# A graph layer on one core: message remainders moved to TensorE, wider comparisons on VectorE, and other edits to a planned schedule

## The chip, the cores and the metric

The kernel runs on one core of a Trainium2 chip. The metric is the time on the device in microseconds (us), the median of several runs. Besides, one execution was recorded by the hardware profiler; the profile's line numbers are those of the kernel's file.

## The reference, cut to what matters

There are 6250 nodes with 128 values each and 100000 edges, sorted by destination. Each edge takes its source's row, multiplies it by one of two weight matrices, according to its type, and adds a bias. The messages are summed by destination, the node's own row times a third matrix is added, and the sum goes through relu, a residual and a layer norm.

```python
Xs = X[src]
m_data = Xs @ W_data.T + b_data
m_ctrl = Xs @ W_control.T + b_control
msg = jnp.where((edge_types == 0)[:, None], m_data, m_ctrl)
agg = jax.ops.segment_sum(msg, dst, num_segments=X.shape[0])
out = agg + (X @ W_self.T + b_self)
x = _layernorm(x + relu(out))
```

## The kernel before, in words

**Blocks.** The nodes are cut into 49 blocks of 128. Sources fall into NT = 98 buckets: 49 blocks for each of the two edge types. A bucket of one destination block has R = 32 slots for its edges; edges beyond that are *spilled* and treated apart.

**First stage: the messages of all nodes.** The messages of every node under both matrices are computed once (`multiply`, L441 the bias, L444 the products), and kept in SBUF as `m3`, in three bf16 parts whose sum has the precision of float32. `split_x` cuts x into three such parts (L420 to L427), so a product takes nine matmuls of 256 columns for a block. The result y stands in PSUM, two blocks to a tile, and is cut into parts by `split_a` to `split_d`: ScalarE copies the first part (L456), VectorE subtracts it from y (L463), ScalarE copies the second (L469), GpSimd or VectorE subtracts again (L474). The table of messages and x's parts are also stored in HBM (`table`, `x3_t`).

**Second stage: where each edge goes.** Blocks are handled in ten groups (four blocks, then five each). For a group, `edge_fields` loads windows of 2304 edges, 18 per partition. For each of the 18 columns k, `bucket_hots` compares the edges' buckets with a count (L544, the tile hot_st); TensorE multiplies that by a triangular matrix (`tri`) into the accumulator `acc`; VectorE takes a maximum over the buckets, which is the edge's rank in its bucket (L561, `slot`); and TensorE adds the rest of the column (`rest`), so that the next column's ranks go on from there. So column k + 1 follows column k through TensorE, VectorE and TensorE. Every three columns (KC = 3), `fill_a` compares the ranks with the 32 slots and multiplies by the source's and destination's place (L574 to L582), and `fill_b` adds these up in PSUM (L600). `fill_c` then copies the filled slots (L613, L615), stores them in HBM (`packed`, L618), turns the destination places (L628, L633), and finds the spilled edges: L640 to L674 pick up to two for each block and partition, L657 and L659 number them, L679 to L699 write a list of up to 32 of them and their one-hot `hot_s`, and L701 fetches their messages from the table. L708 to L718 note whether a bucket or list ran over; then a second, general path follows that the given inputs don't take.

**Third stage: the sums.** For each block, `spread` broadcasts its slots from HBM over all partitions (rows, L733, four buffers), `select` turns them into a one-hot (L740), and `to_hots` makes one for the destinations, five sets at a time (DC = 5, L752, hot_d). Twenty-five times per block, four buckets at a time, `gather` fetches messages by matmul (L768, 128 columns by 384 in four side by side), ScalarE copies them out of PSUM (L777), and `add_up` sums them into the block's accumulator `agg` (L216). The last set has two buckets only, so 64 rows. `own_of` adds the node's own term, one set more the spilled edges. The accumulator has one PSUM buffer: the next block's sums start when `finish_parts` has reduced it (L139). `normalise` scales a group at its end, and stores it.

**The order of the work.** The kernel writes each engine's queue by hand, through a planner (`Order`): every piece of work is a `step` with an assumed cost for each engine that can do it, the steps it needs, and a due time from `due`. The planner takes, among the steps that can start about first, the one due earliest, and emits it. So assumed costs and due times decide the fixed order in which each engine gets its instructions; on the chip every engine goes through its own in that order. BUILT and BLOCK set the due times. `close_build` frees the first stage's SBUF and PSUM, after which the tiles of the third stage are allocated there, the rows among them: their load needs the step `built`.

Of the kernel before, what the change touches and what calls it, by code (L numbers as in the profile page):

```python
# [9 lines left out]
F32 = mybir.dt.float32  # L10
# [9 lines left out]
P = 128  # L20
D = 128
# [18 lines left out]
NC = 4 * NS  # L40
PARTS = (4, 8, 8, 8, 8, 8, 5)
KC = 3
DC = 5
# [54 lines left out]
def kernel(  # L98
# [38 lines left out]
    def finish_parts(h, agg, xs, work):  # L137
        whole = work.tile([P, D], F32, name="whole")
        nc.vector.tensor_reduce(whole, agg.rearrange("p (i c) -> p c i", i=3), axis=AX.X, op=ALU.add)  # L139
        finish(h, whole, xs)  # L140
# [51 lines left out]
    with ExitStack() as main:  # L192
        sums_over_windows(main, tc, x, xt, edges, w, bias, table, x3_t, packed, total,
                          finish_parts, load_rows, norm)
# [6 lines left out]
def sums_over_windows(ctx, tc, x, xt, edges, w, bias, table, x3_t, packed, total,  # L201
                      finish_parts, load_rows, norm):
# [3 lines left out]
    work = ctx.enter_context(tc.tile_pool(name="work", bufs=2))  # L206
    ps_a = ctx.enter_context(tc.tile_pool(name="ps_a", bufs=1, space=PSUM))
# [13 lines left out]
    w_sb = const.tile([D, D3], F32, name="w_sb")  # L221
    A.dma_start(w_sb, w)
    b3 = const.tile([3, D3], F32, name="b3")
    A.dma_start(b3, bias.to_broadcast([3, D3]))
# [22 lines left out]
    V.tensor_scalar_add(slot_f, iota_f[:, :R], 256.0)  # L247
# [19 lines left out]
    early = ctx.enter_context(ExitStack())  # L267
    build = early.enter_context(tc.tile_pool(name="build", bufs=2))
    ps_y = early.enter_context(tc.tile_pool(name="ps_y", bufs=YB, space=PSUM))
# [6 lines left out]


    tri = const.tile([P, P], BF16, name="tri")
    rest = const.tile([P, P], BF16, name="rest")
    tri_f = work.tile([P, P], F32, name="tri_f", bufs=1)  # L280
    V.tensor_scalar(tri_f, iota_f[:, :P], pid, None, op0=ALU.is_gt)
    V.scalar_tensor_tensor(tri_f, ident, 256.0, tri_f, op0=ALU.mult, op1=ALU.add)
    V.tensor_copy(tri, tri_f)
    V.tensor_scalar(rest, tri_f, -1.0, 1.0, op0=ALU.mult, op1=ALU.add)
    ident_b = const.tile([P, P], BF16, name="ident_b")
    V.tensor_copy(ident_b, ident)

    slot_values = []
    for i in range(2):
        vs = const.tile([P, (Q + 1) // 2, NC], BF16, name=f"vs{i}")  # L290
        V.memset(vs, 0.0)
        slot_values.append(vs)
    fifth = const.tile([P, 2, Q], F32, name="fifth")
    for i in range(2):
        V.tensor_scalar_add(fifth[:, i, :], iota_f[:, :Q], 1.0)
# [9 lines left out]
    left = work.tile([D, D3], F32, name="left", bufs=1)  # L305
    three_parts([w3[:, i, :] for i in range(3)], w_sb, left)
    parts = work.tile([3, 3, D3], BF16, name="parts", bufs=1)
    three_parts([parts[:, i, :] for i in range(3)], b3, left[:3])


    spill_tiles = []
    for i in range(2):
        hot = const.tile([P, Q * P], BF16, name=f"hot_s{i}")
        V.memset(hot, 0.0)
        V.memset(hot[R : R + 1, :], 1.0)
        msg = const.tile([P, D3], BF16, name=f"msg_s{i}")
        V.memset(msg, 0.0)
        V.tensor_copy(msg[R : R + 1, :].rearrange("p (i c) -> p i c", i=3), parts[0:1, :, 2 * D :])
        spill_tiles.append((hot, msg))
    bias3 = const.tile([3, D3], BF16, name="bias3")  # L320
    V.tensor_scalar_mul(left[:3], parts[:, 0, :], ident[:3, 0:1])
    for i in (1, 2):
        V.scalar_tensor_tensor(left[:3], parts[:, i, :], ident[:3, i : i + 1], left[:3],
                               op0=ALU.mult, op1=ALU.add)
    V.tensor_copy(bias3, left[:3])
    order.free["V"] = 7.0

    first = const.tile([1, NB], I32, name="first")
    counts = const.tile([P, NPG], F32, name="counts")
    win = const.tile([P, NB, KT, 3], I32, name="win")  # L330
# [3 lines left out]
    def starts():  # L334
        yield step("counted", {"V": 1.8}, lag=0.3)
        dst_f = build.tile([NB, ER], F32, name="dst_f", bufs=1)
        V.tensor_copy(dst_f, er[:, :, 1])
        less = build.tile([NB, ER], F32, name="less", bufs=1)
        in_row = work.tile([NB, 1], F32, name="in_row")
        V.tensor_scalar(less, dst_f, bound_p, None, op0=ALU.is_lt, op1=ALU.add, accum_out=in_row)  # L340
# [7 lines left out]
        for b in range(NB):  # L348
            grp = [g for g in range(NPG) if STARTS[g] <= b][-1]
            yield step(("win", b), {"S": 0.84}, "first", *([("fields", grp - 2)] if grp > 1 else []),  # L350
                       lag=2.0)
            at = nc.values_load(
# [4 lines left out]
                win[:, b, :, :], edges[ds(at, WIN), :].rearrange("(p k) c -> p k c", p=P)  # L357
# [3 lines left out]
    x3s, xts, ys, lefts = {}, {}, {}, {}  # L361
# [6 lines left out]
    BLOCK = 13  # L368
    AHEAD = 12.0

    def due(kind, *i):
# [10 lines left out]
        if kind in ("y", "yh", "yr", "ym", "yl"):  # L382
            return LEAD + each * i[0] + ("y", "yh", "yr", "ym", "yl").index(kind)
        if kind in ("table", "x3_t"):
            return LEAD + each * (at_part[i[0]] + PARTS[i[0]]) + 6
        if kind in ("win", "xs", "agg", "o", "sum"):
# [4 lines left out]
            return begun + (BLOCK + 1 if kind == "sum" else 0.3 * BLOCK)  # L391
        if kind in ("rows", "sel", "d", "g", "e", "s"):
            of = {"rows": 1, "sel": 1, "d": 5}.get(kind, NS)
# [3 lines left out]
        end = BUILT + BLOCK * STARTS[i[0]] - AHEAD  # L397
        begun = end - BLOCK * n
        if kind == "fields":
            return begun - 8  # L400
        if kind in ("hot", "tri", "rank", "rest"):
            return begun + BLOCK * n * i[1] / KT + {"hot": -4, "tri": 0, "rank": 0.5, "rest": 1}[kind]
# [577 lines left out]
```

## Time and profile before

| | |
|---|---|
| time, median of 3 runs | 758.0 us (757.65 to 758.0) |
| span of the profiled execution | 755.7 us |
| TensorE matmuls busy | 694.5 us, 92% |
| TensorE weight loads busy | 553.7 us, 73% |
| VectorE busy | 645.1 us, 85% |
| ScalarE busy | 563.0 us, 74% |
| GpSimd busy | 58.5 us, 8% |
| first / last gather (L768) | 116.5 us / about 743 us |
| DMA | 73.09 MB, a mean of 97 GB/s |

PE is TensorE's matmuls and PEld its weight loads, DVE VectorE, ACT ScalarE, POOL GpSimd, SP the engine that issues most DMAs. A line of a group gives its source line, engine, operation, what it writes from what, the shape and count, then busy time and mean ns of one, and the idle time of the engine just before it with what ended that idle time. "issue" stands for a wait that the profile doesn't explain. Matmuls overlap in pipeline and in the four column strips of the array, so a busy TensorE isn't one at its peak; what tells more is the time from one set's start to the next one's.

### The profile page before, as it was taken

Reading aid. Unit: us, or ns where it says so; the run is one execution under the profiler, and the core shown is the slowest. Engines: PE = TensorE matmul, PEld = TensorE weight load, DVE = VectorE, ACT = ScalarE, POOL = GpSimd, SP = SyncE. Lnnn points to the kernel's source line nnn. Section 1 sums busy time; section 2 is a strip of 40 time slices with the busy share of each in tenths; the row PEclk is TensorE's granted clock in tenths of the full one; section 3 lists DMA queues with packets and bytes.
Section 4 is the critical chain, followed back from the end, with each engine's and each line's share of the span. In section 5 each row is a group of like instructions: output and inputs, shape, how many; then the busy total and the mean of one; then the engine's idle time right before and its main releaser. Section 6 shows DMA issues by size and latency. Waiting matters only on the chain.

```text
span 755.7 us, 34248 instructions
## 1 busy us (share of the span) xinstructions
PE 694.5 (92%) x14578; PEld 553.7 (73%) x14578; DVE 645.1 (85%) x1683; ACT 563.0 (74%) x1379; POOL 58.5 (8%) x48
## 2 busy tenths in 40 slices
PE   0989948999999999999999999999999999999993
PEld 0556636787887888788688778868878887888772
DVE  8798878999999989999999999899989999968531
ACT  1545425788888888778887878878787887789994
POOL 2454420000000000000000000000000000000000
PEclk9999977999999999999999999999999999999997
DMA  5456564024105213410521431052042014105200
GB/s 206 126 175 189 173 199 153 19 82 140 59 21 188 77 23 104 157 27 16 185 77 29 157 102 24 23 195 63 18 183 82 12 53 168 65 12 189 71 4 22
DMA packets 57572, 73.09 MB, mean 97 GB/s; under 512 B 12294, under 2 KB 50195, under 8 KB 57363
## 3 DMA queue, kind: packets, MB, share of 16 engines
q1 hardware_dynamic: 55806, 66.70, 27.2%
q10 hardware_dynamic: 1158, 3.41, 1.3%
q8 instruction: 116, 1.90, 1.0%
q0 software_dynamic: 448, 0.72, 0.3%
q14 instruction: 44, 0.36, 0.2%
HBM read 52.85 MB, written 17.96 MB: 94 GB/s over the span
## 4 chain that ended last, share of the span: by engine, by line
PE 66%; DVE 28%; DMA 2%; issue 2%; ACT 1%; POOL 0%; ACTq 0%; DVEq 0%
PE agg L216 24%; PE g_ps L768 20%; PE acc L216 9%; PE small L600 6%; PE y L444 6%; DVE slot L561 4%; DVE hot_d L752 4%; DVE hot_st L544 2%; DVE two L582 2%; DVE whole L139 2%; DMA rows<-packed 1%; DVE hr L577 1%; DVE rows L740 1%; PE y L441 1%; DVE st L149 1%
## 5 line engine op out<-in xcount | busy, mean ns | idle before, releaser
L777 ACT CAST gs<-g_ps 128x384 bf16<-128x384 f32 x1225 | 493.8, 500 | 114.2 <-PE g_ps L768 79.5
L768 PE MATMUL g_ps<-m,rows 128*32 128x384 bf16 x4802 | 412.1, 331 | 5.9 <-DVE rows L740 5.9
L216 PE MATMUL agg<-gs,hot_d 128*32 128x384 bf16 (+1 forms) x4900 | 412.7, 331 | 1.8 <-ACT gs L777 1.6
L768 PEld LDWEIGHTS <-rows 128*32 128x32 bf16 x4802 | 241.3, 136 | 41.8 <-issue 15.3
L216 PEld LDWEIGHTS <-hot_d 128*32 128x32 bf16 (+1 forms) x4900 | 225.8, 115 | 37.9 <-issue 21.0
L752 DVE TENSOR_TENSOR hot_d<-count,to 128x640 bf16<-128x640 bf16 x245 | 133.0, 553 | 13.6 <-PE agg L216 10.9
L561 DVE TENSOR_REDUCE slot<-acc 128x5 f32<-128x490 f32 (+1 forms) x180 | 116.8, 649 | 17.3 <-PE acc L216 11.4
L544 DVE TENSOR_TENSOR hot_st<-count,st_b 128x640 bf16<-128x640 bf16 (+1 forms) x180 | 100.0, 573 | 0.5 <-PE small L600 0.5
L216 PE MATMUL acc<-hot_st,rest 128*32 128x490 bf16 (+1 forms) x720 | 82.6, 375 | 12.2 <-DVE slot L561 10.8
L216 PE MATMUL acc<-hot_st,tri 128*32 128x490 bf16 (+1 forms) x720 | 89.8, 371 | 2.7 <-DVE full L708 2.7
L600 PE MATMUL small<-hot_st,two 128*32 128x100 bf16 x1764 | 76.1, 294 | 3.4 <-DVE two L582 2.6
L600 PEld LDWEIGHTS <-two 128*32 128x32 bf16 x1764 | 62.9, 119 | 10.6 <-DVE two L582 9.2
L444 PE MATMUL y<-w,x 128*128 128x256 bf16 x441 | 59.7, 282 | 0.4 <-POOL x L427 0.4
L139 DVE TENSOR_REDUCE whole<-agg 128x128 f32<-128x384 f32 x49 | 27.2, 555 | 38.3 <-PE agg L216 29.7
L701 POOL DMA_INDIRECT msg_s<-table,row_i x10 | 13.3, 1330 | 573.9 <-PE g_ps L768 507.8
L216 PEld LDWEIGHTS <-rest 128*32 128x32 bf16 x720 | 32.8, 97 | 28.3 <-issue 25.4
L740 DVE TENSOR_SCALAR rows<-rows,pid 128x3136 bf16<-128x3136 bf16 x49 | 50.4, 1028 | 0.2
L444 PEld LDWEIGHTS <-x 128*128 128x128 bf16 x441 | 39.9, 100 | 12.2 <-POOL x L427 0.9
L216 PE MATMUL agg<-w,x_p 128*32 128x384 bf16 x588 | 37.2, 326 | 0.0
L469 ACT CAST m<-yr 128x512 bf16<-128x512 f32 (+1 forms) x25 | 15.2, 609 | 26.9 <-DVE yr L463 26.7
L216 PEld LDWEIGHTS <-tri 128*32 128x32 bf16 x720 | 30.3, 97 | 6.0 <-issue 4.0
L582 DVE TENSOR_TENSOR two<-hr,lo 128x480 bf16<-128x480 bf16 (+1 forms) x60 | 29.0, 484 | 2.1
(140 smaller groups left out, 462.0 us busy)
## 6 DMA issues: line engine op xcount, KB each, us to landing
rows<-packed SPq DMA_DIRECT2D x49, 784.0 KB, 6.7
table<-m SPq DMA_DIRECT2D x10, 768.0 KB, 7.1
x_p<-x_t SPq DMA_DIRECT2D x49, 96.0 KB, 2.3
x_t<-x SPq DMA_DIRECT2D x5, 768.0 KB, 4.6
xs_p<-in_x SPq DMA_DIRECT2D x49, 64.0 KB, 2.1
xt<-in_xt ACTq DMA_DIRECT2D x5, 512.0 KB, 5.9
out<-h_p SPq DMA_DIRECT2D x8, 320.0 KB, 2.5
win<-in_edges SPq DMA_DIRECT2D x49, 27.0 KB, 2.1
```

What stands on the lines that cost most here:

```text
L139: nc.vector.tensor_reduce(whole, agg.rearrange("p (i c) -> p c i", i=3), axis=AX.X, op=ALU.add)
L216: T.matmul(out[c : c + 32], lhsT[:, c : c + 32], rhs, **flags)
L444: T.matmul(y[:, j, :], x3s[g][:, b + j - at_part[g], i, :], w3[:, k, : 2 * D], start=False, stop=i == k == 2)
L469: A.copy(parts_of(b, n)[1], lefts[b])
L544: V.tensor_tensor(hot, counted[n], fields[grp][2][:, k, None, :].to_broadcast([P, P, n]), op=ALU.is_equal)
L561: V.tensor_reduce(slots[grp][:, k, :], by_q, axis=AX.X, op=ALU.max)
L582: V.tensor_tensor(two[:, :, i], hr, f[:, ks, None, :].to_broadcast(wide), op=ALU.mult)
L600: T.matmul(vt[c0 : c0 + R, q // 2, :], two[:, k - c * KC, i, :, q], hot[:, :, q], start=k == 0 and q < 2, stop=k == KT - 1, skip_group_che ...
L740: V.tensor_scalar(rows[b], rows[b], pid1, None, op0=ALU.is_equal)
L752: V.tensor_tensor(hot, counted[DC], places[grp][:, q, None, c * DC : c * DC + DC].to_broadcast([P, P, DC]), op=ALU.is_equal)
L768: T.matmul(g_ps[t * R : (t + 1) * R, :D3], rows[b][:, :, 4 * g + t], m3[:, 4 * g + t, :], start=True, stop=True)
L777: (A.copy if e == "A" else V.tensor_copy)(gs[:n], g_tiles.pop((b, g))[:n, :D3])
```

## The change

The edits, in the order of the program:

- **Constants and bias.** The bias row is cut into three parts on one partition and spread to a tile of 128 rows, so that its matmul has 128 rows like the others (before: three). The constants are made in a planned step (`constants`) behind the first x remainder. `win` gets two buffers in place of one tile for all blocks; w and other early tiles lie in the pool that is freed.
- **Remainders on TensorE.** `take` and `leave` replace `split_a` to `split_d`: after each part is copied by ScalarE straight from PSUM, TensorE subtracts it there by a matmul with minus the identity. VectorE and GpSimd have no part in it any more. x's third part is always VectorE's.
- **Wide comparisons.** hot_st is made for six columns at once (KC = 6) and for the 98 buckets alone, hot_d for 13 or 12 sets at once (DC = 13), with one count of 13.
- **bf16 ranks.** Ranks count from SLOT = 128 in place of 256, so that they and the slots are exact in bf16, and `at` falls away. The last column's `rest` isn't computed.
- **Spilled edges by the eight largest.** One comparison and one instruction for the eight largest codes of a partition replace the reductions for two per block; eight flags for up to ten; the reduction of `acc` falls away.
- **The last gather of a block** repeats a bucket to fill four, so all sets have 128 rows.
- **The sums' PSUM freed early.** `finish_parts` is cut into `whole` (the reduction out of PSUM) and `sum`; the plan lets the next accumulator start after `whole`.
- **Rows in their own pool**, so their load doesn't need `built`.
- Planned costs and due times are changed throughout (BLOCK 13.5 for 13, group 0 is due 12 us earlier).

The core of the diff:

```diff
-KC = 3
-DC = 5
+RB = 4
+M = 8
+SLOT = 128.0
+KC = 6
+DC = 13
...
+    row_pool = ctx.enter_context(tc.tile_pool(name="row_pool", bufs=RB))
...
-            free = [("yr", two_blocks[i - YB][1])] if i >= YB else []
-            yield step(("y", b), {"T": 1.2 * n}, ("x3", g), *free)
+            free = [("yl", two_blocks[i - YB][1])] if i >= YB else ["biased"]
+            yield step(("y", b), {"T": 1.08 * n}, ("x3", g), *free)
...
-                T.matmul(y[:, j, :], ones_b[:3, :], bias3[:, : 2 * D], start=True, stop=False)
+                T.matmul(y[:, j, :], ones_b, bias3, start=False, stop=True, skip_group_check=True)
...
+    def take(i, kind, after):
         for g, b, n in two_blocks:
+            yield step((kind, b), {"A": 0.16 + 0.21 * n}, (after, b))
+            A.copy(part_of(b, n, i), ys[b][:, :n, :].rearrange("p b (t c) -> p t b c", t=2))
+
+    def leave(i, kind, after):
         for g, b, n in two_blocks:
+            yield step((kind, b), {"T": 0.11 * n}, (after, b))
+            for j in range(n):
+                T.matmul(ys[b][:, j, :].rearrange("p (t c) -> p t c", t=2), minus,
+                         m3v[:, :, b + j, i * D : (i + 1) * D], start=False, stop=True,
+                         skip_group_check=True)
...
-            V.tensor_tensor(hot, counted[n],
-                            fields[grp][2][:, k, None, :].to_broadcast([P, P, n]), op=ALU.is_equal)
+            V.tensor_tensor(hot, counted[n][:, None, 1 : NT + 1, :].to_broadcast([P, KC, NT, n]),
+                            fields[grp][2][:, c * KC : c * KC + KC, None, :].to_broadcast([P, KC, NT, n]),
+                            op=ALU.is_equal)
...
+                if k == KT - 1:
+                    break
                 yield step(("rest", grp, k), {"T": 0.21}, ("rank", grp, k))
...
-                at = work.tile([P, KC, Q], BF16, name="at")[:, :, :n]
-                V.tensor_scalar_add(at, slots[grp][:, ks, :], -256.0)
...
+                V.tensor_tensor(hr, slot_b[n][:, None, :, :].to_broadcast(wide),
+                                slots[grp][:, ks, None, :].to_broadcast(wide), op=ALU.is_equal)
...
+            V.scalar_tensor_tensor(over.rearrange("p (k q) -> p k q", q=n), slot, SLOT + R, code,
+                                   op0=ALU.is_ge, op1=ALU.mult)
+            last = work.tile([P, M], F32, name="last", bufs=1)
+            V.max(last, over)
...
-            V.tensor_reduce(full, accs.pop(grp)[:, : n * NT], axis=AX.X, op=ALU.max)
...
-            yield step(("rows", b), {"S": 0.1}, ("packed", grp), "built", *free, lag=4.0)
-            rows[b] = late.tile([P, R, NT], BF16, name="rows", bufs=RB)
+            yield step(("rows", b), {"S": 0.1}, ("packed", grp), *free, lag=4.0)
+            rows[b] = row_pool.tile([P, R, NT], BF16, name="rows")
...
+            hot = late.tile([P, P * DC], BF16, name="hot_d", bufs=DB)[:, : P * n]
+            d_hots[b, c] = hot = hot.rearrange("p (s g) -> p s g", g=n)
+            V.tensor_tensor(hot, counted[DC][:, :, :n],
+                            places[grp][:, q, None, c * DC : c * DC + n].to_broadcast([P, P, n]),
                             op=ALU.is_equal)
...
-            for t in range(n // R):
-                T.matmul(g_ps[t * R : (t + 1) * R, :D3], rows[b][:, :, 4 * g + t],
-                         m3[:, 4 * g + t, :], start=True, stop=True)
+            for t in range(4):
+                s = min(4 * g + t, NT - 1)
+                T.matmul(g_ps[t * R : (t + 1) * R, :D3], rows[b][:, :, s], m3[:, s, :],
+                         start=True, stop=True)
...
-            yield step(("agg", b), {"S": 0.0}, *([("sum", blocks[i - 1])] if i else []))
+            yield step(("agg", b), {"S": 0.0}, *([("whole", blocks[i - 1])] if i else []))
```

## The prediction

> **What bounds the kernel now.** First the busy tenths over the span (page, part 2), one digit per fortieth:
>
> ```profile
> PE   0989948999999999999999999999999999999993
> ...
> DVE  8798878999999989999999999899989999968531
> ACT  1545425788888888778887878878787887789994
> POOL 2454420000000000000000000000000000000000
> PEclk9999977999999999999999999999999999999997
> ```
>
> TensorE is nearly always busy, but VectorE is too (645.1 of 755.7 us). TensorE has one hole, its sixth slice (94 to 113 us); at the end VectorE is free and ScalarE full. The view by windows of 20 us (TensorE, weight loads, VectorE, ScalarE, GpSimd, clock, DMA) gives the hole and a steady stretch:
>
> ```profile
> 100.00:120.00 20.00, 7.63 (x123) 4.31 (x124) 17.93 (x54) 4.06 (x10) 2.97 (x3) 0.62 0.82 268
> ...
> 280.00:300.00 20.00, 20.00 (x501) 17.87 (x494) 18.26 (x57) 17.56 (x46) 0.00 (x0) 1.00 0.21 62
> ```
>
> Three engines are close together, so I asked what TensorE waits for (waits view: who for whom, us in total, times, longest):
>
> ```profile
> PEld L216 <- issue: 59.0, 182, 2.7
> ...
> PEld L441 <- issue: 11.2, 49, 0.4
> ...
> PE acc L216 <- DVE slot L561: 10.8, 21, 2.0
> ...
> PE g_ps L768 <- DVE rows L740: 5.9, 10, 1.6
> ```
>
> VectorE's lateness shows directly (16.7 us), and TensorE also loses time changing tile shape at L441. Then the timeline, at the hole and at a block's end:
>
> ```profile
> 110.12 1.97 SPq L733 DMA_DIRECT2D rows<-packed  x4
> ...
> 115.37 1.03 DVE L740 TENSOR_SCALAR rows<-rows,pid 128x3136 bf16<-128x3136 bf16 x1
> ...
> 116.50 1.18 PE L768 MATMUL g_ps<-m,rows 128*32 128x384 bf16 x12 [1.60 <-DVE rows L740]
> ```
>
> ```profile
> 303.03 0.12 PEld L216 LDWEIGHTS <-hot_d 64*32 64x32 bf16 x4 [0.28 <-issue]
> ...
> 303.33 0.10 PEld L216 LDWEIGHTS <-hot_s 128*32 128x32 bf16 x4 [0.17 <-issue]
> ```
>
> The first gather waits for its row broadcast, and each block loses time at its 64-row set. The weightiest VectorE groups (busy and mean | idle before):
>
> ```profile
> L752 DVE TENSOR_TENSOR hot_d<-count,to 128x640 bf16<-128x640 bf16 x245 | 133.0, 553 | 13.6 <-PE agg L216 10.9
> L561 DVE TENSOR_REDUCE slot<-acc 128x5 f32<-128x490 f32 (+1 forms) x180 | 116.8, 649 | 17.3 <-PE acc L216 11.4
> L544 DVE TENSOR_TENSOR hot_st<-count,st_b 128x640 bf16<-128x640 bf16 (+1 forms) x180 | 100.0, 573 | 0.5 <-PE small L600 0.5
> ```
>
> In the timeline these follow one another at 0.47, 0.58 and 0.47 us start to start. A comparison of 480 elements (L577, L582) comes after 0.37. So 640 − 480 elements cost 0.10 us; I use 0.13 + elements/1920.
>
> **One group of five blocks, before.** The starts of hot_s (L699) repeat every 64.8 us (235.5, 300.3, 365.2). Work at full flow, from start to start in the timeline: 250 sets of gathers and sums at 0.16 (four matmuls of 384 columns run side by side) = 40.0; own terms and spilled edges 20 sets, 3.2; ranks 36 × 0.204 = 7.3; 180 small ones at 0.031 (24 in 0.74 us at 98.62) = 5.6; the 40 of the lists 1.2. Sum 57.3. The other 7.5 us, read off as excess between neighbours' starts in one group: rank sums waiting for L561, 2.1; the half-filled set and the shape changes about it, 1.8; the new accumulator waiting for L139, 1.3; the first rows of a group, 1.1; flow just short of 0.16, 1.2.
>
> **What the Trainium skill says.** "TensorEngine Tiling (Array Packing)", Key Properties: changing the tiling mode drains TensorE. The trace agrees: 0.28 and 0.17 us above, 0.225 us per block around the 3-row bias matmul. "Advanced Engine Details and Errata", VectorE Performance Modes: two 16-bit elements per cycle want unit step and a start on 4 bytes. The trace agrees only in part: L752 reads slices of `to` that start on odd elements and every one still takes its 0.47. It doesn't show the first operand misaligned, as `counted` from element 5 will be. "SBUF — State Buffer", Who interferes with whom: VectorE and GpSimd share a port pair, held for a whole instruction. It agrees: L544 took 1.74 us at 38.66, beside L427 on GpSimd, against 0.55 alone. "TensorE: Matmul & The Clock Gate", Part 1: after an idle stretch the array runs at half rate. It agrees: clock 0.62 in the hole, and sets at 0.32 us from 117 to 121.
>
> **The change, part by part: the start.** Before, L444 starts at 18.9: VectorE makes all constants first, its first x remainder (L423) runs at 18.25. Afterwards only w's three parts stand ahead of it: minus the 9 us from L299 of the bias to L342, it runs at about 9, and y starts at about 10.5. GpSimd's larger count (1664 elements for 640, 1.83 us before, so some 4.8) delays the first index load from 5.9 to about 9.5; it took 9.8 us to land, so 19, which the longer run of y hides.
> TensorE up to the first gather: 490 matmuls of y and bias × 0.107 = 52.4; new, 98 subtractions × 0.107 = 10.5; ranks 35 × 0.163 and 11 × 0.204 = 8.0; small 4.5; lists 1.3; shape changes at 22 rank clusters × 0.2 = 4.4 (the bias no longer makes any: −11.0, which pays for the subtractions); half rate at first 4; waits for VectorE or ScalarE 4 (before: 4.4). From 10.5 this gives 99.6. ScalarE has 75 copies × 0.53 + 13 of casts = 53 us in these 85: hidden. VectorE loses L463 (17) and GpSimd L427 and L474, hence also the collisions.
> The last small matmul comes some 9 us before, at 90: then copies 0.8, packed stored 2.7, two table stores issued ahead 0.9, rows landing 5.2 as before or up to 9 beside 1.5 MB of table (I take 7.5), select 1.0. First gather at 103, for 116.5: −13.5. Rows in their own pool no longer wait for the end of the table; that edit's worth is in this sum.
> **A group afterwards.** VectorE: hot_d 25 × 0.47 = 11.8 becomes 5 × (1.00 + 0.93) = 9.7; hot_st 18 × 0.47 = 8.5 becomes 3 × 1.66 = 5.0; L574 to L582 6 × 1.43 = 8.6 becomes 3 × 1.9 = 5.7; spilled edges 6.5 (359.0 to 368.9 without the hot_d) become 4.4: eight fewer tiny ones and no L708. With L520 −10.8 us. Bounds: nothing, or 4.6 us more if hot_st goes at one element per cycle (3 × 3.2). TensorE: the half-filled sets become full (+0.4 of work), L600 keeps its 180, one rest set less −0.2, lists −0.1: 57.4. Waits: shape changes 0 for 1.8; accumulator 1.3 still (L139 comes ahead on the list, the hardware wait was for it alone); first rows 0.6; flow 1.3; ranks 0.7 for 2.1, since VectorE has 11 us of room, though a rank reduction may now stand behind one of 1.0 or 1.66 us instead of 0.47. Sum 61.3, or 3.5 less per group.
> ScalarE needs 125 × 0.37 + 3 = 49 us per group: not the bound. Weight loads from rows (136 ns) already hide under 160 ns; those of hot_d, now at a stride of 13, should stay under that. bf16 ranks change no duration.
> **The sum.** First gather 103.0; the first four blocks took 57.2 up to their spilled sums (134.1, 149.3, 161.0, 173.7), less 3.5 and about 2 of half rate: 52, so 155; seven groups × 61.3: 584; an eighth 64.1 − 3: 645; the last blocks are set by ScalarE (10.0 each): 52 − 1, so 696; tail as before 11.8: 708; the runs stand 2.3 above the span (758.0 for 755.7): 710, with some lateness I haven't seen, 711.
>
> **Rivals.** (1) *Only the start gains.* The coarse comparisons hold up the ranks as much as the load did: the group stays at 64.4. 758 − 13.5 − 2 − 9 × 0.4 = 739. For it: the ranks wait on single instructions ahead of them, not on the load; 3.2 us if misalignment halves the rate. Against: the built program's order puts 1 to 3 us of other matmuls between most pairs of tri and rest, and only 0.58 plus its waits is needed. (2) *More gain.* VectorE's waits vanish, group 59.5, first gather 99: 711 − 8.5 × 1.8 − 4 = 692. For: ScalarE and VectorE both have room. Against: the accumulator wait lasts as long as L139. (3) *Slower.* All wide comparisons at one element per ns: hot_d 18.0, hot_st 9.6, hr and two 10.2: VectorE, now 59 of 64.8 us, rises by 6 beyond today's and with gaps sets 68 per group: 758 − 14 + 8.5 × 3.2 = 771. Against: L544 and L577, broadcast in the same way, run at two.
>
> **How the numbers follow.** Forecast 0.62 (702 to 724), rival 1 0.19, rival 2 0.11, slower 0.06, within 0.2% 0.02. Range 695 to 741: it takes in rivals 1 and the upper part of 2 and leaves out some 0.15. Faster 0.92.
>
> **What would show it, and what would make it wrong.** First matmul of y near 10 to 11 and first gather near 103; TensorE without a hole of over 4 us; hot_st at 1.66 us start to start (3.2 means half rate); hot_s every 61 to 62 us; no wait at the set ahead of hot_s; VectorE about 47 of 61 us. Wrong if waits for slot grow beyond 2 us per group, if copies out of y's PSUM hold TensorE in the first 90 us, or if rows land later than 9 us.

## The result, and the profile after

The changed kernel takes 720.9 us (718.8 to 723.9) against 758.0: a ratio of 0.951, 95% interval 0.947 to 0.955. The forecast was 711, the range 695 to 741. Faster was right, and the time lies in the range, 10 us above the forecast. That it came so near is partly luck: as the experiments show, two of its terms were wrong in opposite directions.

The changed kernel's busy tenths, one digit per fortieth of the span:

```profile
PE   3799979999999999999989989999999999999993
...
DVE  8565568788869958886985888699689778657321
ACT  3666546889789887888978888898889888798994
...
PEclk9999989999999999999999999999999999999997
```

VectorE now has room nearly everywhere (74% of the span, before 85%). TensorE's hole, the sixth slice, has 7 tenths for 4, and the granted clock only dips to 8 tenths. The view by windows of 20 us (TensorE, weight loads, VectorE, ScalarE, GpSimd, clock, DMA share, GB/s), for the same two stretches as before:

```profile
100.00:120.00 20.00, 14.52 (x285) 9.84 (x288) 14.40 (x28) 8.46 (x22) 0.87 (x1) 0.83 0.77 263
280.00:300.00 20.00, 18.89 (x449) 15.72 (x444) 17.12 (x36) 17.13 (x45) 0.00 (x0) 1.00 0.60 203
```

From 100 to 120 us TensorE is busy twice as long as before. From 280 to 300 it is idle for 1.1 us, where it was never idle before (a wait for own terms, x_p, at 285.8), and no engine is busy all the time: new waits have come. The waits view (who for whom, us in total, times, longest):

```profile
PE acc L220 <- DVE slot L565: 13.2, 18, 2.7
...
DVE h_p L138 <- DMA out<-h_p: 4.8, 6, 1.7
...
DVE h_p L138 <- ACT gs L760: 4.1, 2, 2.6
...
PE agg L220 <- DMA x_p<-x_t: 3.6, 3, 1.6
...
PE g_ps L752 <- DVE rows L725: 2.8, 1, 2.8
```

The wait for rank reductions (L565), which the lighter VectorE was to shorten, is longer than before (13.2 for 10.8 us). And L138, the end of a block, waits for the store of the outputs, which the kernel before never did. The groups of instructions answering those of before (busy and mean | idle before):

```profile
L565 DVE TENSOR_REDUCE slot<-acc 128x5 bf16<-128x490 f32 (+1 forms) x180 | 117.5, 653 | 78.7 <-PE acc L220 76.1
L739 DVE TENSOR_TENSOR hot_d<-count,to 128x1664 bf16<-128x1664 bf16 x98 | 104.6, 1068 | 11.4 <-PE agg L220 9.1
...
L548 DVE TENSOR_TENSOR hot_st<-count,st_b 128x2940 bf16<-128x2940 bf16 (+1 forms) x30 | 58.8, 1964 | 16.0 <-PE small L603 8.1
```

The timeline at the first gather (start, duration, and in brackets the idle time before and what ended it), from three engines' answers:

```profile
96.32 4.78 SPq L718 DMA_DIRECT2D rows<-packed  x4
```
```profile
104.72 1.04 DVE L725 TENSOR_SCALAR rows<-rows,pid 128x3136 bf16<-128x3136 bf16 x1 [2.80 <-DMA rows<-packed]
```
```profile
105.81 1.18 PE L752 MATMUL g_ps<-m,rows 128*32 128x384 bf16 x12 [2.83 <-DVE rows L725]
```

The first gather still waits for the rows, but starts 10.7 us earlier (105.8 for 116.5). At the end of a block the two idle times of 0.28 and 0.17 us at the 64-row weights are gone.

Where the 38.6 us of span (755.7 to 717.1) came from, by the starts of TensorE's matmuls with hot_s, the last of a block: 10.7 to the first gather; 3.3 in the first four blocks (53.9 for 57.2); 24.5 in eight groups (61.7 us each in the mean, for 64.8); 0.1 in the last five blocks and the tail. But the groups are not alike: 61.4, 60.9, 62.5, 63.9, 62.3, 60.6, 61.3, 60.8, where those of before were level (64.1 to 65.0).

### The profile page after: what moved, and what is told of

The parts are those of the page before. It is cut to its first block, busy times and chain, and to the rows that moved or that the text cites. A ratio compares the mean times of both kernels' runs of the same rounds, so it can differ in the third digit from the quotient of the medians.

```text
span 717.1 us, 33878 instructions
## 1 busy us (share of the span) xinstructions
PE 667.4 (93%) x14698; PEld 574.3 (80%) x14698; DVE 527.5 (74%) x1101; ACT 572.6 (80%) x1407; POOL 23.3 (3%) x21
## 4 chain that ended last, share of the span: by engine, by line
PE 57%; DVE 24%; DMA 10%; ACT 3%; issue 3%; SPq 1%; DVEq 0%; ACTq 0%
PE agg L220 21%; PE g_ps L752 17%; PE acc L220 7%; PE small L603 5%; DVE slot L565 4%; DMA x_p<-x_t 4%; DMA out<-h_p 4%; PE y L461 4%; DVE hot_d L739 4%; DVE hot_st L548 3%; DVE two L586 3%; ACT h_p L179 2%; DVE rows L725 1%; DVE hr L581 1%; PE y L480 1%
## 5 line engine op out<-in xcount | busy, mean ns | idle before, releaser
L220 PE MATMUL agg<-gs,hot_d 128*32 128x384 bf16 x4900 | 407.1, 332 | 2.8 <-ACT gs L760 1.9
L752 PE MATMUL g_ps<-m,rows 128*32 128x384 bf16 x4900 | 399.9, 328 | 3.1 <-DVE rows L725 2.8
L220 PEld LDWEIGHTS <-hot_d 128*32 128x32 bf16 x4900 | 232.5, 137 | 28.4 <-issue 5.9
L752 PEld LDWEIGHTS <-rows 128*32 128x32 bf16 x4900 | 217.0, 137 | 22.6 <-issue 5.6
L565 DVE TENSOR_REDUCE slot<-acc 128x5 bf16<-128x490 f32 (+1 forms) x180 | 117.5, 653 | 78.7 <-PE acc L220 76.1
L739 DVE TENSOR_TENSOR hot_d<-count,to 128x1664 bf16<-128x1664 bf16 x98 | 104.6, 1068 | 11.4 <-PE agg L220 9.1
L220 PE MATMUL acc<-hot_st,rest 128*32 128x490 bf16 (+1 forms) x680 | 72.8, 375 | 13.7 <-DVE slot L565 13.2
L548 DVE TENSOR_TENSOR hot_st<-count,st_b 128x2940 bf16<-128x2940 bf16 (+1 forms) x30 | 58.8, 1964 | 16.0 <-PE small L603 8.1
L473 ACT CAST m<-y 128x512 bf16<-128x512 f32 (+1 forms) x75 | 40.5, 580 | 31.7 <-PE y L464 23.8
L603 PE MATMUL small<-hot_st,two 128*32 128x98 bf16 x1764 | 64.9, 291 | 0.0
L725 DVE TENSOR_SCALAR rows<-rows,pid 128x3136 bf16<-128x3136 bf16 x49 | 50.2, 1024 | 4.0 <-DMA rows<-packed 3.9
L142 DVE TENSOR_REDUCE whole<-agg 128x128 f32<-128x384 f32 x49 | 27.1, 553 | 34.6 <-PE agg L220 33.3
L220 PEld LDWEIGHTS <-x_p 128*32 128x32 bf16 x588 | 20.7, 97 | 9.2 <-DMA x_p<-x_t 5.4
L220 PEld LDWEIGHTS <-tri 128*32 128x32 bf16 x720 | 24.5, 97 | 2.8 <-issue 2.1
```

The lines of the kernel that those rows point to most:

```text
L220: T.matmul(out[c : c + 32], lhsT[:, c : c + 32], rhs, **flags)
L473: A.copy(part_of(b, n, i), ys[b][:, :n, :].rearrange("p b (t c) -> p t b c", t=2))
L548: V.tensor_tensor(hot, counted[n][:, None, 1 : NT + 1, :].to_broadcast([P, KC, NT, n]), fields[grp][2][:, c * KC : c * KC + KC, None, :].t ...
L565: V.tensor_reduce(slots[grp][:, k, :], by_q, axis=AX.X, op=ALU.max)
L603: T.matmul(vt[c0 : c0 + R, q // 2, :], two[:, k, i, :, q], hot[:, k, :, q], start=c == k == 0 and q < 2, stop=c * KC + k == KT - 1, skip_g ...
L725: V.tensor_scalar(rows[b], rows[b], pid1, None, op0=ALU.is_equal)
```

## The experiments

In each kernel's trace the excess of TensorE over full flow was added up over eight groups: from one set's start to the next, less 0.040 us for each matmul of 384 columns, 0.051 for the ranks', 0.031 for the small ones. It is put down to what came next; the ranks' second half is `rest`, which needs a rank reduction. How neighbours are taken together moves some 0.4 us between sums and gathers (0.9 before, and up to 2 with the sums freed late, where the ranks move too); the columns of ranks and spilled edges stay within 0.1 in the other rows. Per group of five blocks, in us (first gather and time are those of the whole kernel):

| kernel | time | first gather | group | ahead of ranks' second half | of sums | of gathers | of spilled edges |
|---|---|---|---|---|---|---|---|
| before | 758.0 | 116.5 | 64.8 | 2.3 | 2.8 | 1.7 | 0.7 |
| changed | 720.9 | 105.8 | 61.7 | 2.8 | 0.9 | 0.8 | 0.1 |
| two h_p buffers | 708.9 | 104.7 | 60.5 | 1.6 | 0.8 | 0.9 | 0.1 |
| + narrow, same places | 725.7 | 107.8 | 62.0 | 3.2 | 0.9 | 0.8 | 0.1 |
| + narrow, planned anew | 704.4 | 102.2 | 60.1 | 1.5 | 0.4 | 0.8 | 0.1 |
| + sums freed late | 732.6 | 105.4 | 63.1 | 2.0 | 3.6 | 0.6 | 0.1 |
| + 64-row sets | 716.4 | 106.0 | 61.1 | 1.2 | 1.4 | 0.9 | 0.9 |
| the best | 692.7 | 100.1 | 59.5 | 1.5 | 0.2 | 0.8 | 0.1 |

(The changed kernel and the one with two h_p buffers have the same order on every engine; their first gathers differ by 1.1 us, so that much is no finding.)

**Two buffers for h_p.** The longest group holds the longest wait for a reduction. VectorE there, then the queue that stores, then TensorE:

```profile
358.31 0.55 DVE L142 TENSOR_REDUCE whole<-agg 128x128 f32<-128x384 f32 x1
358.78 0.66 DVE L565 TENSOR_REDUCE slot<-acc 128x5 bf16<-128x490 f32 x1
362.04 0.29 DVE L138 SCALAR_TENSOR_TENSOR h_p<-whole,xs_p 128x128 f32<-128x128 f32 x1 [2.60 <-ACT gs L760]
```
```profile
357.03 0.39 SPq L186 DMA_DIRECT2D out<-h_p  x1
```
```profile
366.79 0.39 PE L220 MATMUL acc<-hot_st,rest 128*32 128x490 bf16 x4 [2.68 <-DVE slot L565]
```

L138 writes the first block of a new group into h_p, of which there is one buffer; its store of the group before was issued at 357.0. L138 waits for several things, and the bracket names ScalarE; but its last L179 on h_p had ended at 357.0, and its load of x, issued at 339.1, had landed 8.9 us later, so that of the things waited for only the store can have been open. Of the next group's store the trace has the landing too: issued at 420.8, it landed 3.9 us later, and L138 started at 424.9. Behind L138 the queue of VectorE is held, a reduction with it, and behind that TensorE's `rest`. "PSUM — Partial Sum Buffer", section "Engine vs sequencer instructions", of the Trainium skill says that VectorE's queue is strict FIFO; the trace agrees: the matmuls of `tri` that the next reduction reads started at 360.67 and took 0.39 us, and it started at 366.07. Between L138 and this reduction stand some 3.7 us of other work, a hot_d and the fields of a later group. With two buffers the same work stands there, and TensorE's `rest` comes without a wait that the view shows; it is the 2.6 us on top that it had no room for.

```diff
-                hs_[grp] = late.tile([P, Q, D], F32, name="h_p")
+                hs_[grp] = late.tile([P, Q, D], F32, name="h_p", bufs=2)
```

> The changed kernel with two buffers for h_p instead of one; the order of instructions on every engine stays. Theory (store holds VectorE, VectorE holds TensorE): in the changed kernel the first L138 of every group stands 1.5 to 3.7 us after its L142 instead of 0.64, because the store of the group before is issued only about 12 us after its last L142, and the rank reduction L565 queued behind it keeps rest waiting 0.8 to 2.9 us once a group, 11 us in the eight groups. Then: time 708 to 713 (720.9 less 8 to 12), hot_s every 60.2 to 60.8 us, all groups alike, L138 0.64 us after L142, and runs within 2 us of one another. Rival one (the reductions stand behind a comparison of 1.0 to 2.0 us anyway): 719 to 721, groups still 61.7. Rival two (own terms and x late behind the row broadcasts make the long groups): 715 to 718, groups of over 62 us remain.

Measured: 708.9 us (707.5 to 710.0), 12 us less than the changed kernel; groups 60.5 in the mean, 60.1 to 61.7 but for the last (58.6). VectorE at the same point, and the waits:

```profile
355.85 0.55 DVE L142 TENSOR_REDUCE whole<-agg 128x128 f32<-128x384 f32 x1
356.31 0.66 DVE L565 TENSOR_REDUCE slot<-acc 128x5 bf16<-128x490 f32 x1
356.89 0.28 DVE L138 SCALAR_TENSOR_TENSOR h_p<-whole,xs_p 128x128 f32<-128x128 f32 x1
```
```profile
PE acc L220 <- DVE slot L565: 2.5, 8, 0.8
```

L138 follows with no gap, its wait is gone from the view altogether, and with it 10.7 of the 13.2 us of TensorE's waits for L565. The hold is shown, and both rivals fall; the wait of up to 1.5 us for own terms (x_p) remains. As this kernel has the changed one's order, the further edits were made on it.

**The sums' PSUM freed late again.** In the kernel before, L135 followed 0.64 us after L139, although h_p had one buffer too. Which edit brought the hold? The natural suspect is the split of the block's end: L142 alone at once, the rest due 3 us later.

```diff
-            yield step(("whole", b), {"V": 0.5}, ("s", b, NS - 1))
-            whole = add_parts(aggs.pop(b), work)
-            yield step(("sum", b), {"V": 0.7}, ("whole", b))
+            yield step(("sum", b), {"V": 1.25}, ("s", b, NS - 1))
+            whole = add_parts(aggs.pop(b), work)
...
-            yield step(("agg", b), {"S": 0.0}, *([("whole", blocks[i - 1])] if i else []))
+            yield step(("agg", b), {"S": 0.0}, *([("sum", blocks[i - 1])] if i else []))
```

> The kernel with two h_p buffers, and the early freeing of the sums' PSUM undone: L142, L138 and the statistics are one step of 1.25 us again, due a block and 1 us after the block's begin, and the next accumulator is planned behind all of it. Theory (the wait for the accumulator, 0.6 us once and 0.2 to 0.5 us in the other blocks of a group before, is gone because the planner now counts on 0.5 us): 0.6 to 1.3 us more per group, 5 to 12 us in all (714 to 721). Rival (the hardware wait was for L142 alone in both, and L142 may even come earlier): within 3 us (706 to 712).

Measured with two buffers: 732.6 us, 23.7 more; twice the theory's upper end, so the forecast's view of this edit (worth nothing) falls, and the theory is short by half. The first sum of a block, which needs the accumulator, now costs 1.4 us per group instead of 0.4; the last four blocks, without ranks beside them, take 10.1 us each instead of 9.8. Most of the rest is another wait, TensorE for ScalarE's copies: 10.5 us in all, for 1.9 with the split. TensorE at one of these:

```profile
231.61 0.50 PE L752 MATMUL g_ps<-m,rows 128*32 128x384 bf16 x8
233.31 0.39 PE L220 MATMUL agg<-gs,hot_d 128*32 128x384 bf16 x4 [1.21 <-ACT gs L760]
```

From 230.85 to 232.9 ScalarE applies the norm to five blocks (L179), and the copies that TensorE wants stand behind. Where the order puts these five is decided by when the sums are planned. This part is read from the trace; it was not tried by itself.

> The changed kernel, h_p with its one buffer, and only the early freeing of the sums' PSUM undone. With two h_p buffers the same edit gave 732.6 us, and its trace has the last L179 of a group at 232.4, the next block's L142 at about 238: the store has some 5.5 us to land there, while the changed kernel leaves it 1.4. Theory (the edit that frees the PSUM early moved the group's statistics, and so the store, behind; it is this that made the single h_p buffer a wait): 731 to 735, as with two buffers; the edit as it stood was then worth about 12 us, and 24 without the wait it brought. Rival (the single h_p buffer costs 12 us with either order): 742 to 746.

Measured with one buffer: 732.1 us. Without the split the second buffer brings nothing (732.1 against 732.6); with it, 12 us. So the split made the single buffer a wait, and it was worth 11 us as it stood and 24 without the wait it brought.

The same edit alone, with two buffers, on the kernel before (its lines there: L139, L135):

> The kernel before, with the early freeing of the sums' PSUM alone (L139 a step of its own of 0.5 us, the rest of the block's end due 3 us after, the next accumulator planned behind L139 only), and two h_p buffers. Theory (the edit's worth doesn't hang on the others: 2.5 us per group): 735 to 745. Rival (in the kernel before VectorE's own load, 59 of 64.8 us, keeps TensorE where it is): 752 to 758.

Measured: 745.6 us for 757.5, ratio 0.985 (0.983 to 0.987); groups 63.5 for 64.8, the last four blocks 9.7 to 9.8 for 9.9 to 10.1. It is worth 12 us there, half of what it is beside the others: nearer the theory, but just short of its range.

**The wide comparisons.** First cut in the old places of the old order, the planner's prices unchanged (L548 into six of 490 elements, shown here, and L739 into three):

```diff
-            V.tensor_tensor(hot, counted[n][:, None, 1 : NT + 1, :].to_broadcast([P, KC, NT, n]),
-                            fields[grp][2][:, c * KC : c * KC + KC, None, :].to_broadcast([P, KC, NT, n]),
-                            op=ALU.is_equal)
+            for k in range(KC):
+                V.tensor_tensor(hot[:, k], counted[n][:, 1 : NT + 1, :],
+                                fields[grp][2][:, c * KC + k, None, :].to_broadcast([P, NT, n]),
+                                op=ALU.is_equal)
```

> The kernel with two h_p buffers, each L548 cut into six comparisons of 490 and each L739 into three of at most 624, in the same places of the same order. VectorE gets 3 x 0.65 + 10 x 0.26 = 4.5 us more work per group of 60. Theory (VectorE has room; single waits, not its load, hold TensorE): at most 0.4 us more per group, 0 to 4 us in all. Rival (VectorE's load sets the waits for slots, as the prediction has it): 1 to 3 us more per group, 9 to 25 us in all.

Measured: 725.7 us, 16.8 more, 1.5 per group and 3.2 before the first gather. By start-to-start times VectorE got only 2.4 us more per group (six at 0.375 for one of 1.91 us; 1.14 for 1.00). One hot_st and what follows it, wide (two h_p buffers) and narrow:

```profile
364.02 2.00 DVE L548 TENSOR_TENSOR hot_st<-count,st_b 128x2940 bf16<-128x2940 bf16 x1
365.93 0.68 DVE L565 TENSOR_REDUCE slot<-acc 128x5 bf16<-128x490 f32 x1
```
```profile
248.32 2.34 DVE L548 TENSOR_TENSOR hot_st<-count,st_b 128x490 bf16<-128x490 bf16 x6
250.57 0.67 DVE L565 TENSOR_REDUCE slot<-acc 128x5 bf16<-128x490 f32 x1
```

Yet the waits view of the narrow one reads:

```profile
PE acc L220 <- DVE slot L565: 14.7, 46, 3.0
```

46 waits, for 8. The rival seemed right: load sets the waits. But load and the plan's error went together here, so the second run undid the width as it had been before: one planned step per column of hot_st, five columns of hot_d at a time.

```diff
-DC = 13
+DC = 5
...
-            yield step(("hot", grp, c), {"V": 0.13 + KC * NT * n / 1920}, ("fields", grp), *free)
...
+                yield step(("hot", grp, c * KC + k), {"V": 0.13 + NT * n / 1920}, ("fields", grp), *free)
```

> The kernel with two h_p buffers, and the wide comparisons undone: hot_st by the column (490 elements), hot_d by five columns, each with a step of its own in the planner, so that the order is planned anew. VectorE gets about 4 us more work per group (hot_st 2.0, hot_d 2.1); reductions may stand between the comparisons. Theory (VectorE's load and what stands ahead of a reduction in its fixed order set the waits for slots, as the run with narrow comparisons in the old places, 16.8 us slower, suggests): 8 to 17 us slower than with two h_p buffers alone (717 to 726). Rival (only what stands ahead of one reduction counts, and a planner that is free to interleave gets it back): within 4 us (706 to 713).

Measured: 704.4 us (703.1 to 707.2), 4.5 less than with the wide ones. VectorE's busy time from 200 to 500 us tells that it has the most work of the three (two h_p buffers, narrow in the old places, narrow planned anew; columns as above):

```profile
200.00:500.00 300.00, 295.44 (x7080) 263.17 (x7074) 247.57 (x518) 260.24 (x661) 7.66 (x5) 1.00 0.28 92
```
```profile
200.00:500.00 300.00, 291.48 (x6913) 257.20 (x6916) 252.20 (x678) 255.83 (x650) 7.66 (x5) 1.00 0.28 92
```
```profile
200.00:500.00 300.00, 295.99 (x7148) 259.41 (x7144) 265.43 (x673) 262.34 (x667) 7.87 (x5) 1.00 0.29 92
```

247.6, 252.2 and 265.4 us: more work than the slowest, and 21 us faster. So VectorE's load did not set the time, and the theory that expected 717 to 726 falls. What is left is the order: the places in it had been chosen for other durations. The new plan differs in more, though: its steps are finer, so that a rank need not wait for six columns at once, and hot_d has eight small buffers for four large ones. What each of these gives was not tried apart. Making the comparisons wide was, on this base, a small loss.

**The 64-row sets back.**

```diff
-            for t in range(4):
-                s = min(4 * g + t, NT - 1)
+            for t in range(min(4, NT - 4 * g)):
+                s = 4 * g + t
```

(and eviction and sum of the last set over those 64 rows)

> The kernel with two h_p buffers, and the last gather of a block back to its two filled quarters: 64-row evictions and sums. Theory of the prediction (changes of tile shape drain TensorE; 1.8 us of waits per group before, less 0.4 us of work saved): 1.2 to 1.5 us more per group than with two h_p buffers alone, 12 to 15 us in all. Rival (TensorE has slack there, since it waits for slots or evictions anyway): 0 to 4 us more in all.

Measured: 716.4 us, 7.6 more. In the profiled executions 4.7 us of it lie in the eight groups (0.6 each), 2.3 in the first four blocks and 1.3 before the first gather, where no such set runs. The weight loads have the old idle times again:

```profile
261.08 0.14 PEld L220 LDWEIGHTS <-hot_d 64*32 64x32 bf16 x4 [0.28 <-issue]
261.40 0.10 PEld L220 LDWEIGHTS <-hot_s 128*32 128x32 bf16 x4 [0.17 <-issue]
```

The mechanism is right, the size between theory and rival: what the full sets save at the change of shape (1.4 per group ahead of sums and spilled edges) is partly spent on 0.4 us of work and on waits for ranks that come back (1.6 for 1.2).

**The start.** Three runs: the count of 13 as a copy on VectorE instead of GpSimd's iota; the rows back in the late pool; the remainders back on VectorE and GpSimd.

```diff
-for n in sorted({DC, *GROUPS}):
+for n in sorted({*GROUPS}):
...
+        V.tensor_copy(counted[DC], iota_f[:, :P, None].to_broadcast([P, P, DC]))
```

> The kernel with two h_p buffers, and the count of 13 made by a VectorE copy among the constants instead of by GpSimd at the start. Theory (GpSimd's iota of 1664 holds the shared port and stretches the first casts of w, L283, to 2.9 us): L283 under 1 us, first matmul of y at 5.5 to 6.5 us instead of 8.4, first gather 2 to 3 us earlier, time 2 to 3 us less than with two h_p buffers alone. Rival (TensorE catches up before 100 us because its own order waits for the slots and the rows): first gather within 0.7 us of before, time within 1 us.

```diff
-            yield step(("rows", b), {"S": 0.1}, ("packed", grp), *free, lag=4.0)
+            yield step(("rows", b), {"S": 0.1}, ("packed", grp), "built", *free, lag=4.0)
```

> The kernel with two h_p buffers, and the rows back in the pool that opens when the first stage is closed: the first four broadcasts stand behind all stores of the table. With the pool of their own they are issued from 95.3 us on, and the last table store at 100.7. Theory (the first gather waits for the chain packed, broadcast, L725): first gather 4 to 7 us later, 108 to 111 instead of 104.7, and the time 4 to 7 us more (713 to 716). Rival (the broadcasts, alone on the queues then, land the sooner, or TensorE's other work is not done by then anyway): within 2 us.

```diff
-        multiply(), take(0, "yh", "y"), leave(0, "y1", "yh"),
-        take(1, "ym", "y1"), leave(1, "y2", "ym"), take(2, "yl", "y2"),
+        multiply(), take(0, "yh", "y"), left_v(), take_left(), last_v(),
```

> The kernel with two h_p buffers, and the remainders of the messages back on VectorE and GpSimd (y less its first part from PSUM into an F32 tile, the second part from there, the third on VectorE or GpSimd). TensorE loses 98 matmuls of 0.107, 10.5 us; VectorE gains 49 blocks of some 0.35 us and part of the third differences, 17 to 30 us before the first gather, and collides with GpSimd again. Theory (VectorE sets the first stage then): first gather 6 to 13 us later (111 to 118), time 6 to 13 us more (715 to 722). Rival (TensorE's 100 us of work set the first stage, VectorE has room): first gather 3 to 9 us earlier, time 700 to 706.

Measured: *count as a copy*: the first cast of w (L284 there) takes 0.34 us instead of 2.88, the first matmul of y comes at 5.9 for 8.4, the first gather 1.6 earlier. Changed kernel, then this one:

```profile
5.48 2.88 DVE L283 CAST w<-w_sb 128x384 bf16<-128x384 f32 x1
```
```profile
5.48 0.34 DVE L284 CAST w<-w_sb 128x384 bf16<-128x384 f32 x1
```

The time, 707.9 (705.6 to 708.2), is 0.9 less, inside the runs' spread: that the iota stretched the cast is shown, what that costs is not. *Rows late*: issued at 102.5, first gather at 109.7, 714.4 us, 5.5 more: as the theory said. *Remainders on VectorE*: first gather at 101.2, 3.5 earlier; 706.5 us (705.8 to 707.7), 2.4 less than 708.9 (707.5 to 710.0), hardly more than the spread. The theory (VectorE sets the first stage) falls, and the rival has the first gather right and the time just outside. From 20 to 100 us, first with the remainders on TensorE, then on VectorE:

```profile
20.00:100.00 80.00, 78.04 (x898) 59.53 (x899) 48.99 (x94) 47.46 (x84) 0.00 (x0) 0.98 0.62 188
```
```profile
20.00:100.00 80.00, 68.10 (x812) 50.50 (x812) 73.63 (x123) 36.66 (x60) 34.03 (x22) 0.98 0.66 203
```

TensorE is the full engine of this stage in the changed kernel; the headline edit put work onto it. VectorE had room for the remainders: it was busy for 49 of these 80 us. The run also frees y's PSUM after the first subtraction instead of at the end; how much that gives was not tried apart.

**Put together.** Two h_p buffers, narrow comparisons planned anew, remainders on VectorE (and no count of 13); then also x_p and x loaded ahead of the rows of their block instead of behind them:

```diff
-            yield step(("xs", b), {"S": 0.9}, ("rows", b), "built", *free, lag=4.0)
+            yield step(("xs", b), {"S": 0.9}, "built", *free, lag=4.0)
...
-            return begun + {"whole": BLOCK + 0.5, "sum": BLOCK + 3}.get(kind, 0.3 * BLOCK)
+            return begun + {"xs": -9.5, "whole": BLOCK + 0.5, "sum": BLOCK + 3}.get(kind, 0.3 * BLOCK)
```

> The changed kernel with two h_p buffers, the comparisons by the column again (and with them no count of 13), and the remainders of the messages on VectorE and GpSimd. If the single gains add up (12.0, 4.5 and 2.4 us, and 0.9 for the count): 700 to 702. If the remainders on VectorE collide with the finer comparisons in the first stage: 703 to 706.

> As the run with all three, and the loads of own terms and x (L781, L147) no longer planned behind the rows of their block but due half a microsecond ahead of them. Theory (x_p lands 7 us after its issue because three row broadcasts of 784 KB stand ahead of it, and TensorE waits for it some 3 to 4 us in all): 2 to 4 us less than without it. Rival (the rows come later instead, and the gathers wait for them): 0 to 5 us more.

Measured: 695.0 (693.1 to 696.4), 6 us better than the sum of the single gains (720.9 less 12.0, 4.5, 2.4 and 0.9 is 701.1). Much of that may be spread: by the spans of the profiled executions the three gains on two h_p buffers are 5.7, 2.3 and 3.2 us, and together they gave 12.7. And 692.7 us (692.4 to 692.8), ratio 0.914 (0.913 to 0.916), the best version. In the latter the loads land in 3.2 us (issue to landing), where they took 7.3 with two h_p buffers alone, and 2.3 in the kernel before:

```profile
x_p<-x_t SPq DMA_DIRECT2D x49, 96.0 KB, 3.2
```
```profile
x_p<-x_t SPq DMA_DIRECT2D x49, 96.0 KB, 7.3
```
```profile
x_p<-x_t SPq DMA_DIRECT2D x49, 96.0 KB, 2.3
```

Own terms stand no more in the waits view of TensorE, as they did not in the kernel before. There these loads didn't need the rows of their block; the change made them need them, an edit that neither the list of the edits nor the forecast names. This run takes it back, and makes the loads due earlier as well.

## Why the prediction was right, point by point

**Start.** y began at 8.4 where 10.5 was forecast, but its first set lost 4.5 us to waits, first for parts of w and then, longer (0.88 and 1.15 us), for parts of x, whose remainder VectorE makes behind the parts of w. The first cast of w ran beside GpSimd's iota: that the iota is long was foreseen for the index load, not for this. TensorE came to the end of its other work at 103.0 (forecast 99.6). The chain of the rows is as named: last small matmul 92.7 (90), rows to L725 8.4 us (7.5), first gather 105.8 (103). The step "the bias no longer makes any, which pays for the subtractions" stands by itself untested; undoing the subtractions gained 2.4 us, so the room they made on VectorE was worth less than they cost. The rows' pool gave 5.5 us.

**VectorE per group.** The forecast took 10.8 us off; its busy time fell by 9.1 (from 59.4 to 50.3: the busy share from 200 to 500 us, times the length of a group). Mis-sized were hot_st, 1.91 instead of 1.66 us start to start, and hr and two, 2.1 instead of 1.9. The price, 0.13 us and 1920 elements per us, comes within 0.01 us of the two readings given for it, but it fails at the length that it was used for. Taken as they stand, 0.47 us for 640 elements and 0.10 less for 480 make 0.07 us and 1600 elements per us, and with these hot_st is 1.91 and hr and two 2.0. The planner had the same price, so its order counted on each hot_st 0.25 us too early. Hot_d was right (1.00). That misaligned operands halve the rate (rival 3) is ruled out: at half rate hot_st was to take 3.2.

**TensorE per group.** Forecast 57.4 of work and 3.9 of waits; measured 61.7, of which 4.6 of waits (the table's four columns), hence 57.1 of work. The sum is nearly right, two terms are wrong. *"Accumulator 1.3 still (L139 comes ahead on the list, the hardware wait was for it alone)"* failed: the waits ahead of a block's first sum fell to 0.4 per group, and the edit costed at nothing was the largest of those undone here. When L142 runs is only half the matter: the planner puts TensorE's and ScalarE's work where it believes the accumulator to be free. *"Ranks 0.7 for 2.1, since VectorE has 11 us of room"* failed too: 2.8, by this measure the sign of being wrong that the prediction had named (above 2). Some 1.2 of it was the hold at L138, a wait that the early freeing of the PSUM made; and in the narrow runs the wait does not go with VectorE's load: 1.6, 3.2 and 1.5 with rising load. *"Shape changes 0 for 1.8"*: they vanished (0.1), but the net worth of the full sets was 0.6 per group. Own terms, not in the forecast, cost 0.3.

**Rivals.** Rival 1 (only the start gains, group 64.4) had the right reason, that ranks wait for single instructions ahead of them and not for load, but the group fell for other reasons. Rival 2's figures (group 59.5, 692 us) are those of the best version, which got there by other edits. Of the 3.1 us per group the split gave some 1.3 net of its hold, the full sets 0.6, width −0.5. About 1.6 are left to edits not separated here: the spilled edges by the eight largest, the coarser hr and two, one rest set less, and what the parts give each other (the split gives 12 or 24 us according to company). The bias of 128 rows, too, was not undone alone.

**Error of 10 us.** 2.8 at the first gather, 1.9 in the first four blocks, 3.6 in the eight groups, 0.9 at the end, 0.8 between the span shown and the median, beyond what the forecast allowed for it and for lateness. Removing the hold gave 12 us, more than all of it.

## What to carry to other kernels

When an edit frees a resource earlier by moving the rest of that step later, look at what the moved part triggers (here a store) and whether its buffer is single; in a FIFO queue that wait holds all that stands behind, and a trace may name another engine. Free room on an engine shortens a wait only if the room lies ahead of the instruction waited for, and with a planned order only if the plan's prices are those of the chip. A rate that fits two near lengths within 0.01 us can be off by 0.25 us at one five times as long. Before moving work to the engine that bounds a stage, price leaving it where it was.

## What the runs showed of the hardware

- A comparison of 2940 elements took 1.91 us start to start, six of 490 took 0.375 each, so one long instruction saved 0.34 us of 2.25. The lengths 490, 640 (0.47, in the kernel before) and 2940 lie on one line, 0.07 us and 0.63 ns per element: long and short go at the same rate, and what is saved is the fixed part, five times. The innermost run has five elements in all of these, 3.1 ns each; runs of 13 (hot_d, 128 of them in 1.00 us) took, less the fixed part, 7.3 ns each.
- The first group has runs of four. In both runs with narrow comparisons its hot_st of 392 elements took 0.27 and 0.375 us in turn: the columns of the second operand lie five elements apart, so every other one starts on an odd element. Runs of five took 0.375 us from an even and from an odd start alike. "Advanced Engine Details and Errata", VectorE Performance Modes, of the Trainium skill lists a start on 4 bytes among the conditions for two 16-bit elements per cycle. Here an odd start cost runs of four half as much again and runs of five nothing, and the measurement decides.
- An estimate that fits all of these is 1.04 ns for each 4-byte word that a run touches: two for four elements from an even start, three for four from an odd one and for any five, seven for 13. It is worked out from these durations and was not tried by itself.
- A cast of 128x384 on VectorE took 2.88 us beside an iota on GpSimd, and 0.34 us without.
- A load of 96 KB landed 7.3 us after its issue behind row broadcasts of 784 KB (two h_p buffers), and 3.2 us when it was issued ahead of them (the best version).
